# Two graph attention layers in one kernel: the product of a finished block's output is issued between the first and the second group of the next block's sums

## The chip, the cores and the metric

The kernel runs on one core of a Trainium2 chip. The metric is the device time of one execution in microseconds (us). The engines of the core work side by side, each through its own queue in order: TensorE (PE in the profile, with its weight loads as PEld), VectorE (DVE), ScalarE (ACT), GpSimd (POOL) and SyncE (SP, which here only issues DMAs). Transfers between the main memory and the on-chip memory run on 16 DMA engines.

## The reference, cut to what matters

A graph of 6250 nodes with 256 features each and 100,000 edges goes through two residual steps. The first step is two GATv2 layers with 4 heads of 64 channels, with one added edge from each node to itself; the second is one GAT layer with 8 heads of 32 channels. In each layer a node takes a softmax over its incoming edges and sums the rows of the source nodes with these weights.

```python
def _gatv2_layer(x, src, dst, n, Wl, Wr, att, b):
    xl = (x @ Wl).reshape(n, H, C)
    xr = (x @ Wr).reshape(n, H, C)
    e = jax.nn.leaky_relu(xl[src] + xr[dst], NEG_SLOPE)
    logits = jnp.einsum('ehc,hc->eh', e, att)
    ...  # softmax over the edges of each dst: alpha
    msg = xl[src] * alpha[:, :, None]
    out = jax.ops.segment_sum(msg, dst, num_segments=n)
    return out.reshape(n, H * C) + b
...
h = elu(_gatv2_layer(x, src, dst, n, Wl1, Wr1, att1, b1))
h = _gatv2_layer(h, src, dst, n, Wl2, Wr2, att2, b2)
x = _layernorm(x + h)
x = _layernorm(x + _L1_gnn_ref(x, W, a, src, dst))
```

All numbers are 32-bit floats.

## The kernel before, in words

**Blocks.** The nodes are sorted by their number of incoming edges and cut into 49 blocks of 128, one node per partition. Block b has `cols[b]` edge columns: 27 in block 0, 25 in block 1, 18 in block 17, 17 in block 18, 15 in block 27, 11 in blocks 44 and 45, 9 in block 48. With the node's own row a block of layers 1 and 2 has S = `cols[b]` + 1 rows of 260 numbers per partition (block 0 a few more, handled apart). These rows are held in tiles `g` of at most 9 rows each, called groups here: block 0 has four, blocks 1 to 17 have three, and blocks 18 to 48 have two, of equal size or one apart (18 = 9 + 9, 16 = 8 + 8, 12 = 6 + 6). There are 9 such tiles (`rowp`), so GpSimd can load some four blocks of two groups ahead.

**Gathers.** One indirect DMA of GpSimd (line 1300) fetches one edge column: 128 rows of the table in main memory. All three layers take 2409 of them. Layer 2 gathers from the table that layer 1 writes, layer 3 from the table that layer 2 writes. So that a layer can begin its gathers early, the sources of its first three blocks are sorted, and 37 gathers (14, 12 and 11 columns, `soon` in the profile) read the table only up to block 44 (`AHEAD`); the gathers after them need all 49 blocks.

**One block of `layer2`** (lines 1635 to 1666; `i` is 0 in layer 1 and 1 in layer 2). Each engine takes its instructions in the order in which the Python code emits them; the order is written out by hand. In iteration b:

1. `start` issues loads for block b + 3, `gather` the gathers of block b + 1.
2. `ready(b + 1)` makes the block's own terms. In layer 1 (`own1`) TensorE turns the block's input (two transposes, line 1420, copied to SBUF by ScalarE, line 1422) and multiplies it with both weight matrices (`pl` and `pr`, line 1427). In layer 2 (`own2`) both have been loaded, and ScalarE copies `pr` (line 1724).
3. `attend(b)`: VectorE makes the logits, three passes for each group (lines 1591, 1594, 1595; the first pass of the first group was made an iteration earlier). ScalarE puts block b + 1's own row in its tile (line 1684 in layer 1, 1725 in layer 2). `weights` takes the maximum on VectorE (line 1439) and four exponentials on ScalarE (line 1446). Then VectorE makes the first pass of block b + 1 (`first_z`, line 1571), which reads `pr` and that own row.
4. `finish(b - 1)` takes the sums of the block before, `acc`, and returns `rest`, which makes the block's output (layer 1: ELU, lines 1689 to 1697; layer 2: a layer norm, lines 1522 to 1534).
5. `weighted_sum(b)`: VectorE multiplies the rows of each group by their weights (line 1483). Of the last group ScalarE takes some columns in place of VectorE, four multiplies to a column (line 1482): S // 3 of them in layer 1 and S // 2 in layer 2, at most the group's rows less one. TensorE adds the rows up in PSUM by matmuls with the identity (line 1490), two instructions to a row. After the first group's multiply `between` calls `rest`.
6. `last[0]()`: the function that `rest` returned turns the finished output of block b - 1 (transposes on TensorE, the copy of line 1422 on ScalarE), multiplies it with the next layer's weights (line 1427), copies the result to `row` (ScalarE, lines 1704, or 1738 and 1739) and issues the DMAs that write the next layer's table rows (SP, lines 1708 and 1709, or 1740).

Layer 3 uses no TensorE sums; its weighting and adding are on VectorE.

In step 5 ScalarE's multiplies of the last group stand ahead of the copies of step 6 in ScalarE's queue, and all matmuls of the block stand ahead of the transposes of step 6 in TensorE's queue:

```python
for g, (s0, s1) in zip(rows, cut):
    ...
    for t in range(m, n):
        for h in range(H):
            nc.scalar.mul(g4[:, t, h, :], g4[:, t, h, :], by[:, t - m, h : h + 1])
    nc.vector.tensor_mul(...)
    if s0 == 0:
        between()
    for t in range(n):
        nc.tensor.matmul(acc, ident, g4[:, t], ...)
```

Of the kernel before, what the change touches and what calls it, by code (L numbers as in the profile page):

```python
# [26 lines left out]
F32 = mybir.dt.float32  # L27
# [8 lines left out]
P = 128  # L36
# [1171 lines left out]
def tile_by_degree(  # L1208
# [3 lines left out]
    nc = tc.nc  # L1212
    N, F = x.shape
    H2, D2 = att1.shape
    H1, _, D1 = w3.shape
    NB = -(-N // P)
    NP = NB * P
    T = 9
    A1 = F + H1
    W2 = H2 * (D2 + 1)  # L1220
# [5 lines left out]
    xl2_d = dram.tile([NP + 1, W2], F32, name="xl2_d")  # L1226
    xr2_d = dram.tile([NP, W2], F32, name="xr2_d")
    wh_d = dram.tile([NP + 1, A1], F32, name="whs_d")

    def per_head(t, H):  # L1230
        return t.rearrange("p (h d) -> p h d", h=H)
# [55 lines left out]
    s2 = consts.tile([P, NB, H1], F32, name="s2_r")  # L1287
# [129 lines left out]
    def transposed(work, ps, xt):  # L1417
        pt = ps.tile([P, 2, P], F32, name="pt", tag="tp")
        for c in range(2):
            nc.tensor.transpose(pt[:, c, :], xt[:, c * P : (c + 1) * P], ident)  # L1420
        xT = work.tile([P, 2, P], F32, name="xT")
        nc.scalar.copy(xT, pt)  # L1422
        return xT

    def product(pm, xT, w):
        for c in range(2):
            nc.tensor.matmul(pm, xT[:, c, :], w[:, c, :], start=c == 0, stop=c == 1)  # L1427
# [33 lines left out]

        return (wt, None), add_up

    def weighted_sum(work, ps, rows, cut, wts, H, width, between, plus, more=False):


        wt, (k0, k1) = wts
        acc = ps.tile([P, F], F32, name="acc")
        S = cut[-1][1]
        by = None  # L1470
        if k1 > k0:
            by = work.tile([P, k1 - k0, H], F32, name="by")
            nc.scalar.copy(by, wt[:, k0:k1, :])  # L1473
        for k, t in enumerate(plus):
            nc.tensor.matmul(acc, ident, t, start=k == 0, stop=False)
        for g, (s0, s1) in zip(rows, cut):
            n = s1 - s0
            g4 = g[:, :n, : H * width].rearrange("p t (h d) -> p t h d", h=H)[:, :, :, : F // H]
            m = n - by.shape[1] if by is not None and s1 == S else n
# [3 lines that stand above are left out]
            nc.vector.tensor_mul(  # L1483
                g4[:, :m], g4[:, :m],
                wt[:, s0 : s0 + m, :].unsqueeze(3).to_broadcast([P, m, H, F // H]),
# [4 lines that stand above are left out]
                nc.tensor.matmul(  # L1490
                    acc, ident, g4[:, t], start=False, stop=s0 + t == S - 1 and not more
                )
        return acc

    def added_up(work, prod, rows, cut, wts, H, width, between):
# [24 lines left out]
    def spread_of(work, t):  # L1520
        stats = work.tile([P, nc.vector.BN_STATS_DIM], F32, name="stats")
        nc.vector.bn_stats(stats, t)  # L1522
        mv = work.tile([P, nc.vector.BN_AGGR_DIM], F32, name="mv")
        nc.vector.bn_aggr(mv, stats)
        sd = work.tile([P, 2], F32, name="sd")
        nc.scalar.activation(sd[:, :1], mv[:, 1:2], AF.Ln, bias=eps)  # L1526
        nc.scalar.activation(sd[:, :1], sd[:, :1], AF.Exp, scale=-0.5)
        return mv, sd
# [7 lines left out]
    def layer2(i, table, of, width, start, own, finish, follow):  # L1536
# [5 lines left out]
        with ExitStack() as es:  # L1542
            zp = es.enter_context(tc.tile_pool(name=f"z{i}", bufs=1))
            work = es.enter_context(tc.tile_pool(name=f"work{i}", bufs=3))
            ps = es.enter_context(tc.tile_pool(name=f"ps{i}", bufs=2, space=PSUM))
            ps1 = es.enter_context(tc.tile_pool(name=f"ps1{i}", bufs=1, space=PSUM))
            pst = es.enter_context(tc.tile_pool(name=f"pst{i}", bufs=2, space=PSUM))
# [4 lines left out]
            def gather(b):  # L1552
                first = EARLY[b] if b in begun else 0
                rows, cut = begun.pop(b) if first else row_tiles(b, 1)
                gather_rows(b, rows, cut, 1, table, of, width, first, cols[b])
                if b == 0:
                    gather_few(table, i, width)
                state[b] = [rows, cut]
# [3 lines left out]
            def ready(b):  # L1562
                pr, put = own(work, ps, pst, b, state[b][0][0][:, 0, :W2])
                state[b].append(pr)
                later.append(put)
# [68 lines left out]
            acc, rest = None, None  # L1634
            for b in range(NB):
                if b + 3 < NB:
                    start(b + 3)
                if b + 1 < NB:
                    gather(b + 1)
                if b + 2 == NB:  # L1640
                    follow()
                if b + 1 < NB:
                    ready(b + 1)
                rows, cut, wt, new = attend(b)
                if b:
                    rest = finish(work, pst, b - 1, acc)
                else:
                    new()
                    few = few_sum(work, pst, wt[0], cols[0] + 1, H2, D2 + 1)
                if b:  # L1650
                    new()

                last = []

                def between():
                    if b:
                        last.append(rest())

                acc = weighted_sum(
                    work, ps, rows, cut, wt, H2, D2 + 1, between,  # L1660
                    [bias[0]] if i == 0 else [x1[:, b, :], bias[1]], b == 0,
                )
                if b == 0:
                    nc.tensor.matmul(acc, edges_of, few, start=False, stop=True)
                if last:
                    last[0]()
            finish(work, pst, NB - 1, acc)()()

    def none(t):

        nc.vector.memset(t.rearrange("p (h d) -> p h d", h=H2)[:, :, D2:], -BIG)
# [14 lines left out]
    def finish1(work, pst, b, acc):  # L1686
        h = work.tile([P, F], F32, name="h")
        neg = work.tile([P, F], F32, name="neg")
        nc.scalar.activation(neg, acc, AF.Relu, scale=-1.0)
        nc.scalar.activation(neg, neg, AF.Exp, scale=-1.0)  # L1690
        pos = work.tile([P, F], F32, name="pos")
        nc.scalar.activation(pos, acc, AF.Relu)

        def rest():
            row = work.tile([P, 2, W2], F32, name="row2")
            none(row[:, 1, :])
            nc.vector.scalar_tensor_tensor(h, neg, -1.0, pos, op0=OP.add, op1=OP.add)

            def last():
                hT = transposed(work, pst, h)  # L1700
                for j in range(2):
                    pm = pst.tile([P, W2], F32, name="pm", tag="tp")
                    product(pm, hT, wc[1][:, j])
                    nc.scalar.copy(
                        per_head(row[:, j, :], H2)[:, :, : W2 // H2 - j],
                        per_head(pm, H2)[:, :, : W2 // H2 - j],
                    )
                nc.sync.dma_start(xl2_d[b * P : (b + 1) * P], row[:, 0, :])
                nc.sync.dma_start(xr2_d[b * P : (b + 1) * P], row[:, 1, :])

            return last

        return rest

# [12 lines left out]
    def finish2(work, pst, b, h):  # L1727
        mv, sd = spread_of(work, h)

        def rest():  # L1730
            layer_norm(x1[:, b, :], h, mv, sd)

            def last():
                hT = transposed(work, pst, x1[:, b, :])
                pm = pst.tile([P, F + 2 * H1], F32, name="pm3", tag="tp")
                product(pm, hT, wh)
                row = work.tile([P, A1], F32, name="row3")
                nc.scalar.copy(row, pm[:, :A1])
                nc.scalar.copy(s2[:, b, :], pm[:, A1:])
                nc.sync.dma_start(wh_d[b * P : (b + 1) * P], row)  # L1740

            return last

        return rest

# [12 lines left out]
    with ExitStack() as es:  # L1758
        work = es.enter_context(tc.tile_pool(name="work3", bufs=3))
        ps = es.enter_context(tc.tile_pool(name="ps3", bufs=3, space=PSUM))  # L1760
# [59 lines left out]
        acc, den, puts, rest = None, None, {}, None  # L1820
        for b in range(NB):
# [4 lines left out]
            rows, cut, wt, new = attend(b)  # L1826
# [5 lines left out]
            def between():  # L1832
                if b:
                    puts[b - 1] = rest()

            acc = added_up(work, prod, rows, cut, wt, H1, D1, between)
            if b == 0:
                more = ps.tile([P, F], F32, name="few_acc", tag="tp")
# [34 lines left out]
```

## Time and profile before

| | us |
|---|---|
| median of 3 runs (lowest to highest) | 3332.04 (3331.96 to 3335.03) |
| the profiled execution, its own time | 3328.12 |
| its span, first to last instruction | 3326.3 |
| layer 1: first gather to the first `soon` gather of layer 2 | 131 to 1212 |
| layer 2: from there to the first `soon` gather of layer 3 | 1212 to 2236 |
| layer 3: from there to the end | 2236 to 3326 |

| engine | busy us | share of the span | instructions |
|---|---|---|---|
| DVE | 2755.3 | 83% | 2527 |
| POOL | 2435.2 | 73% | 2588 |
| PE | 1416.2 | 43% | 5423 |
| ACT | 1108.0 | 33% | 4428 |

The 2409 gathers take 0.946 us each as POOL's busy time, and 0.30 us lie between two of them, so that one starts every 1.25 us at best. The mean granted clock of TensorE is 0.711 of full speed over the span. A row of a timeline gives the start, the time taken, the engine, the line, the operation, `out<-in`, the number of instructions merged in it, and in brackets the engine's idle time before it with what ended that idle time.

### The profile page before, as it was taken

What the parts mean: (1) busy time and instruction counts of PE and PEld (TensorE: products, weight loads), DVE (VectorE), ACT (ScalarE), POOL (GpSimd) and SP (SyncE); (2) the same over time, 40 slices, a digit from 0 to 9 for tenths busy, and PEclk for the clock granted to TensorE, in tenths of its full rate; (3) what the DMA queues carried; (4) which work ended last, traced back from release to release, by engine and by line L of the source; (5) the groups of instructions that cost most, each with busy time, mean ns of one, the idle gap of its engine ahead of it and who ended that gap; (6) DMA issues with size and microseconds to landing.
All of it is one profiled execution on the core that took longest, in us unless ns stands there. A gap on an engine that the chain in (4) does not pass through costs nothing.

```text
span 3326.3 us, 24261 instructions
## 1 busy us (share of the span) xinstructions
PE 1416.2 (43%) x5423; PEld 1131.0 (34%) x5424; DVE 2755.3 (83%) x2527; ACT 1108.0 (33%) x4428; POOL 2435.2 (73%) x2588
## 2 busy tenths in 40 slices
PE   7346666666677773565656666662000000000000
PEld 5235554555555552454545454552000000000000
DVE  7599998889888888999999999985966767666766
ACT  3134434444444442444445666561000000000000
POOL 5477777777777767777777777767777777777776
PEclk8678888888888886777877878886555555555555
DMA  8744444444444444444444444444333333333333
GB/s 198 145 111 118 117 118 121 118 120 122 121 121 121 124 111 112 122 121 127 121 127 126 132 126 132 131 111 115 108 107 107 108 108 107 108 107 107 107 107 86
DMA packets 189103, 395.84 MB, mean 119 GB/s; under 512 B 56249, under 2 KB 107963, under 8 KB 188934
## 3 DMA queue, kind: packets, MB, share of 16 engines
q0 software_dynamic: 121392, 339.19, 39.0%
q1 hardware_dynamic: 59858, 53.27, 5.7%
q10 hardware_dynamic: 7700, 1.74, 0.5%
q8 instruction: 47, 0.77, 0.1%
q14 instruction: 106, 0.87, 0.1%
HBM read 354.02 MB, written 40.42 MB: 119 GB/s over the span
## 4 chain that ended last, share of the span: by engine, by line
POOL 23%; DVE 15%; issue 13%; PE 7%; DMA 3%; ACT 1%; DVEq 0%; POOLq 0%; ACTq 0%
POOL g L1300 22%; PE acc L1490 6%; DVE g L1483 3%; DVE z L1594 3%; DVE lg L1595 3%; DVE z L1571 3%; DVE z L1591 2%; DMA g<-xl_d,near_r 1%; POOL out L1812 1%; DMA out<-y,node_i 1%; PE pm L1427 1%; DVE stats L1522 0%; DMA g<-whs_d,near_r 0%; ACT sd L1526 0%; DVE weighted L1503 0%
## 5 line engine op out<-in xcount | busy, mean ns | idle before, releaser
L1300 POOL DMA_INDIRECT g<-xl_d,near_r x1569 | 1484.4, 946 | 485.8 <-issue 434.8
L1490 PE MATMUL acc<-g,ident 128*128 128x256 f32 x3408 | 972.0, 455 | 654.2 <-DVE g L1483 357.6
L1490 PEld LDWEIGHTS acc<-g,ident 128*128 128x128 f32 x3408 | 788.8, 235 | 838.3 <-DVE g L1483 378.4
L1300 POOL DMA_INDIRECT g<-whs_d,near_r x766 | 727.1, 949 | 233.3 <-issue 227.2
L1482 ACT ACTIVATE g<-g,by 128x64 f32<-128x64 f32 x2308 | 561.0, 336 | 1.6
L1595 DVE TENSOR_REDUCE lg<-z 128x28 f32<-128x1820 f32 (+4 forms) x234 | 497.4, 2125 | 8.1
L1594 DVE TENSOR_TENSOR z<-z,at 128x1820 f32<-128x1820 f32 (+4 forms) x234 | 496.9, 2124 | 4.7
L1483 DVE TENSOR_TENSOR g<-g,wt 128x1792 f32<-128x1792 f32 (+8 forms) x234 | 331.8, 1435 | 31.9 <-ACT by L1473 31.9
L1512 DVE TENSOR_REDUCE acc_v<-weighted 128x256 f32<-128x4096 f32 (+15 forms) x49 | 343.7, 7014 | 1.6
L1591 DVE TENSOR_TENSOR z<-g,pr 128x1820 f32<-128x1820 f32 (+3 forms) x138 | 299.6, 2171 | 23.2 <-DMA g<-xl_d,near_r 14.8
L1456 ACT ACTIVATE wt<-lg 128x128 f32<-128x128 f32 (+17 forms) x49 | 14.0, 285 | 803.6 <-DVE lg L1455 803.6
L1782 DVE TENSOR_TENSOR lg<-g,s_r 128x56 f32<-128x56 f32 (+4 forms) x111 | 22.4, 214 | 268.5 <-DMA g<-whs_d,near_r 212.2
L1571 DVE TENSOR_TENSOR z<-g,pr 128x2080 f32<-128x2080 f32 (+4 forms) x96 | 197.9, 2061 | 44.5 <-DMA g<-xl_d,near_r 13.5
L1503 DVE TENSOR_TENSOR weighted<-g,wt 128x1792 f32<-128x1792 f32 (+4 forms) x111 | 226.6, 2057 | 0.1
L1422 ACT COPY xT<-pt 128x256 f32<-128x256 f32 x147 | 55.0, 374 | 505.8 <-PE pt L1420 505.8
L1446 ACT ACTIVATE wt<-lg,top 128x19 f32<-128x19 f32 (+14 forms) x392 | 115.7, 295 | 234.2 <-DVE top L1439 224.7
L1427 PE MATMUL pm<-wcat,xT 128*128 128x260 f32 x392 | 99.0, 395 | 22.6 <-ACT xT L1422 22.6
L1427 PEld LDWEIGHTS pm<-wcat,xT 128*128 128x128 f32 x392 | 70.4, 189 | 42.8 <-ACT xT L1422 34.3
L1446 ACT ACTIVATION_READ_ACCUMULATOR wt<-lg,top 128x1 f32 x392 | 73.5, 187 | 0.0
L1812 POOL DMA_INDIRECT out<-y,node_i x49 | 50.1, 1022 | 25.8 <-issue 14.2
L1427 PE MATMUL pm<-wh_cat,xT 128*128 128x272 f32 x196 | 59.0, 424 | 22.6 <-ACT xT L1422 22.6
L1427 PE MATMUL pl<-wcat,xT 128*128 128x260 f32 x196 | 57.2, 415 | 25.2 <-ACT xT L1422 25.2
(250 smaller groups left out, 1527.3 us busy)
## 6 DMA issues: line engine op xcount, KB each, us to landing
g<-xl_d,near_r POOLq DMA_INDIRECT x1569, 2.8
g<-whs_d,near_r POOLq DMA_INDIRECT x766, 2.8
whs_d<-row SPq DMA_DIRECT2D x49, 132.0 KB, 2.0
xl_d<-xl SPq DMA_DIRECT2D x49, 130.0 KB, 7.9
xl_d<-row SPq DMA_DIRECT2D x49, 130.0 KB, 2.6
xr_d<-row SPq DMA_DIRECT2D x49, 130.0 KB, 2.9
two<-xl_d SPq DMA_DIRECT2D x49, 130.0 KB, 2.9
two<-xr_d SPq DMA_DIRECT2D x49, 130.0 KB, 3.3
```

The lines of the kernel that those rows point to most:

```text
L1300: nc.gpsimd.indirect_dma_start(out=g[:, j + own - s0, :width], out_offset=None, in_=table, in_offset=source(of, b, j),)
L1427: nc.tensor.matmul(pm, xT[:, c, :], w[:, c, :], start=c == 0, stop=c == 1)
L1446: nc.scalar.activation(wt[:, :, h], lg[:, :S, h], AF.Exp, bias=top[:, h : h + 1], accum_out=den[:, h : h + 1],)
L1482: nc.scalar.mul(g4[:, t, h, :], g4[:, t, h, :], by[:, t - m, h : h + 1])
L1483: nc.vector.tensor_mul(g4[:, :m], g4[:, :m], wt[:, s0 : s0 + m, :].unsqueeze(3).to_broadcast([P, m, H, F // H]),)
L1490: nc.tensor.matmul(acc, ident, g4[:, t], start=False, stop=s0 + t == S - 1 and not more)
L1503: nc.vector.tensor_mul(prod[:, s0 - base : s1 - base, :].rearrange("p t (h d) -> p t h d", h=H), g[:, :n, :F].rearrange("p t (h d) -> p t ...
L1512: nc.vector.reduce_sum(part, prod[:, : s1 - base, :].rearrange("p s f -> p f s"), axis=AX.X)
L1571: nc.vector.tensor_max(z, rows[0][:, :n, :W2], xr[:, None, :].to_broadcast([P, n, W2]))
L1591: nc.vector.tensor_max(z, g[:, :n, :W2], xr[:, None, :].to_broadcast([P, n, W2]))
L1594: nc.vector.tensor_mul(z, z, at[:, None, :].to_broadcast([P, n, W2]))
L1595: nc.vector.reduce_sum(lg[:, s0:s1, :], z.rearrange("p t (h d) -> p t h d", h=H2), axis=AX.X)
```

## The change

The function that `rest` returned did all of step 6. It is cut in two. The first part, `turn`, holds the transposes, the copy to SBUF and the products; it is called by a new `middle`, which `weighted_sum` calls after the first group's matmuls. The second part, `last`, holds the copies to `row` and the DMAs, and stays where step 6 was, after all groups. In layer 1 each of the two DMAs is now issued directly after its own copy. The last block of a layer calls all parts in turn. No operation is added or removed.

```diff
@@ weighted_sum
+    def weighted_sum(work, ps, rows, cut, wts, H, width, between, middle, plus, more=False):
...
                 nc.tensor.matmul(
                     acc, ident, g4[:, t], start=False, stop=s0 + t == S - 1 and not more
                 )
+            if s0 == 0:
+                middle()
         return acc
@@ layer2
+                def middle():
+                    if b:
+                        last.append(last.pop()())
+
                 acc = weighted_sum(
-                    work, ps, rows, cut, wt, H2, D2 + 1, between,
+                    work, ps, rows, cut, wt, H2, D2 + 1, between, middle,
...
                 if last:
                     last[0]()
-            finish(work, pst, NB - 1, acc)()()
+            finish(work, pst, NB - 1, acc)()()()
@@ finish1
-            def last():
+            def turn():
                 hT = transposed(work, pst, h)
+                made = []
                 for j in range(2):
                     pm = pst.tile([P, W2], F32, name="pm", tag="tp")
                     product(pm, hT, wc[1][:, j])
-                    nc.scalar.copy(
-                        per_head(row[:, j, :], H2)[:, :, : W2 // H2 - j],
-                        per_head(pm, H2)[:, :, : W2 // H2 - j],
-                    )
-                nc.sync.dma_start(xl2_d[b * P : (b + 1) * P], row[:, 0, :])
-                nc.sync.dma_start(xr2_d[b * P : (b + 1) * P], row[:, 1, :])
-
-            return last
+                    made.append(pm)
+
+                def last():
+                    for j, (pm, to) in enumerate(zip(made, (xl2_d, xr2_d))):
+                        nc.scalar.copy(
+                            per_head(row[:, j, :], H2)[:, :, : W2 // H2 - j],
+                            per_head(pm, H2)[:, :, : W2 // H2 - j],
+                        )
+                        nc.sync.dma_start(to[b * P : (b + 1) * P], row[:, j, :])
+
+                return last
+
+            return turn
@@ finish2
-            def last():
+            def turn():
                 hT = transposed(work, pst, x1[:, b, :])
                 pm = pst.tile([P, F + 2 * H1], F32, name="pm3", tag="tp")
                 product(pm, hT, wh)
-                row = work.tile([P, A1], F32, name="row3")
-                nc.scalar.copy(row, pm[:, :A1])
-                nc.scalar.copy(s2[:, b, :], pm[:, A1:])
-                nc.sync.dma_start(wh_d[b * P : (b + 1) * P], row)
-
-            return last
+
+                def last():
+                    row = work.tile([P, A1], F32, name="row3")
+                    nc.scalar.copy(row, pm[:, :A1])
+                    nc.scalar.copy(s2[:, b, :], pm[:, A1:])
+                    nc.sync.dma_start(wh_d[b * P : (b + 1) * P], row)
+
+                return last
+
+            return turn
```

More of the change, by code (lines that the diff above doesn't have):

```diff
@@ L1462, in weights @@
         return (wt, None), add_up
-    def weighted_sum(work, ps, rows, cut, wts, H, width, between, plus, more=False):
+    def weighted_sum(work, ps, rows, cut, wts, H, width, between, middle, plus, more=False):
         wt, (k0, k1) = wts
```

## The prediction

> **What bounds the kernel now.** I read the page's groups first, then POOL's waits. The page's costliest group is the gathers; its columns are busy time, mean ns of one, and the idle time before them with what ended it.
>
> ```profile
> L1300 POOL DMA_INDIRECT g<-xl_d,near_r x1569 | 1484.4, 946 | 485.8 <-issue 434.8
> ```
>
> All 2409 gathers at 0.946 + 0.30 us make 3.0 ms of the 3.3 ms span, so GpSimd nearly never rests. What another engine costs must show as a wait of GpSimd. In its waits (total us, times, longest), "issue" is only the steady 0.30 us; two single waits stand out:
>
> ```profile
> POOL g L1300 <- PE pl L1427: 17.2, 2, 16.9
> ...
> POOL g L1300 <- DVE stats L1522: 14.1, 3, 13.5
> ```
>
> The timeline places them at 1211.98 and 2235.97: each is the first `soon` gather of the next layer, which needs block 44's table row. The names of the releasers are inferred; the row itself is on SP, 2.7 us before:
>
> ```profile
> 2233.26 0.32 SPq L1740 DMA_DIRECT2D whs_d<-row  x1
> ...
> 2235.97 0.95 POOL L1300 DMA_INDIRECT g<-whs_d,soon  x1 [13.48 <-DVE stats L1522]
> ```
>
> With 2.5 us at 1260.69 (block 48's row) and 3.7 us at 1302.81 (a free tile), GpSimd waits 36.6 us for the other engines after its start. That is the most that any speed-up here can give; a slow-down is not limited. Layer 3 starts when block 44's row of layer 2 lands, and gathers without a break after that. So the question is when that row lands.
>
> The table by stages (length; PE, PEld, DVE, ACT, POOL busy; clock) tells who sets that: layer 1 from block 27, layer 2's three-group blocks, its two-group blocks, layer 3.
>
> ```profile
> 850.00:1244.00 394.00, 278.14 (x1044) 220.30 (x1044) 331.17 (x293) 187.71 (x764) 285.39 (x302) 0.86 0.45 119
> 1292.00:1736.00 444.00, 257.17 (x960) 208.26 (x960) 430.88 (x324) 185.84 (x765) 333.41 (x353) 0.78 0.45 122
> 1736.00:2236.00 500.00, 319.52 (x1142) 253.75 (x1142) 468.78 (x395) 301.45 (x1252) 368.01 (x391) 0.80 0.47 127
> 2282.00:3326.00 1044.00, 2.68 (x6) 1.50 (x6) 730.59 (x772) 68.00 (x197) 778.49 (x819) 0.50 0.39 106
> ```
>
> In layer 2 VectorE is busy 97% and 94% of the time, and a block's gathers end 24 to 39 us before its weights are ready (timeline, block by block), so GpSimd's lead is not used up: VectorE's chain sets layer 2, and each microsecond added to it arrives at 2235.97. In layer 1 VectorE waits about 2 us a block for TensorE (line 1671, 45.7 us in 20 waits): there TensorE's chain sets the pace. VectorE's waits in layer 2's two-group blocks:
>
> ```profile
> DVE g L1483 <- ACT by L1473: 9.9, 29, 0.4
> DVE z L1571 <- ACT g L1725: 8.5, 13, 1.5
> DVE z L1571 <- DMA g<-xl_d,near_r: 5.7, 5, 1.4
> ```
>
> Only line 1571, which needs ScalarE's copy of line 1725, can change. ScalarE's timeline of one block (27), whose sums run on TensorE from 1914.96 to 1924.58 and whose transposes follow at 1924.42, shows how near that copy is:
>
> ```profile
> 1915.53 6.78 ACT L1482 ACTIVATE g<-g,by 128x64 f32<-128x64 f32 x28
> 1924.83 0.37 ACT L1422 COPY xT<-pt 128x256 f32<-128x256 f32 x1 [2.52 <-PE pt L1420]
> 1926.48 0.38 ACT L1738 COPY row<-pm 128x264 f32<-128x264 f32 x1 [1.27 <-PE pm L1427]
> 1926.76 0.17 ACT L1739 COPY s_r<-pm 128x8 f32<-128x8 f32 x1
> 1926.81 0.40 ACT L1724 COPY pr<-two 128x260 f32<-128x260 f32 x1
> 1927.12 0.42 ACT L1725 COPY g<-two 128x260 f32<-128x260 f32 x1
> ```
>
> and on VectorE:
>
> ```profile
> 1926.98 0.27 DVE L1439 TENSOR_REDUCE top<-lg 128x4 f32<-128x64 f32 x1
> 1927.58 2.32 DVE L1571 TENSOR_TENSOR z<-g,pr 128x2080 f32<-128x2080 f32 x1 [0.33 <-ACT g L1725]
> ```
>
> ScalarE weights from 1915.5 to 1922.3 beside the sums, then stands idle 2.5 us for the transposes. That idle time is the cover of the weighting. The copy of line 1725 ends at 1927.54, 0.2 us after VectorE could use it (line 1439's end + 0.1).
>
> **The change, part by part.** No work comes or goes; two queues are reordered.
>
> *ScalarE, layer 2.* The copy of line 1422 moves ahead of the last group's multiplies. It waits for transposes that stand behind the first group's matmuls; 28 multiplies, two `row` copies, `pr` and the copy of line 1725 queue behind it. How long the first group takes is read from the sums' rows (PE busy, PEld busy, then PEclk):
>
> ```profile
> 1914.90:1919.70 4.80, 4.74 (x11) 3.81 (x12) 0.50 0.39 100
> 1919.90:1924.30 4.40, 4.40 (x22) 3.78 (x20) 0.99 0.37 97
> ```
>
> The sums begin at half clock, 0.427 us an instruction, and change to 0.216 us. Over all blocks that takes 2.7 to 6.1 us, about 4.4: nearly always inside the first group. Here the first group's 16 instructions end 6.0 us after the start at 1914.96, not at half of 9.6. Then: 0.42 to the copy (1924.42 to 1924.83), 0.32 to the first multiply (spacing of ScalarE's short copies), 28 x 0.2425 = 6.8 (6.78 for 28), 1.1 from the last multiply to the end of line 1725's copy (1926.48 to 1927.54, and 0.04). Sum 6.0 + 0.42 + 0.32 + 6.8 + 1.1 = 14.6; now it is 12.6. VectorE is ready at 12.4, so it waits 2.3 instead of 0.2: **2.1 us lost** in this block.
>
> The same sum with each block's own rows, blocks 18 to 45: S 18: 2.4 (4 blocks), 17: 2.2 (5), 16: 1.9 (5), 15: 1.8 (5), 14: 1.5 (4), 13: 1.5 (3), 12: 1.0 (2); together 9.6 + 11 + 9.5 + 9 + 6 + 4.5 + 2 = 51.6 us. Longer blocks meet the clock at other points: its change falls on a fixed grid of 3.41 us (the first fast matmuls of 45 blocks lie within 0.3 us of it). Played forward block by block on that grid, the loss is 44 to 48, depending on the start; I take 46. Without the change the same replay ends 0.1 us from the trace's last block.
>
> Three-group blocks lose nothing: block 10's copy would end 12.6 us after the sums begin, VectorE needs it at 18.7. Their cover is the third group's passes on VectorE (lines 1591, 1594 and 1595, 1.78 to 2.05 us each); where it is gone, from block 18 on, the loss begins.
>
> *TensorE, layer 2.* Transposes and products go first; the second group then runs at ScalarE's pace (0.97 a row against 0.43). `acc` is done some 4 us later, still 2 us ahead of line 1522. The second group's tile is released as much later; GpSimd is 24 us or more ahead.
>
> *Layer 1.* TensorE's chain to `pr` keeps its length: sums, two transposes, the 0.46 us for ScalarE's copy, products (2.0), own transposes, `pl`, `pr`. ScalarE must weight before TensorE needs its rows: with S 16 the last of 20 multiplies (0.32 + 4.88) ends 5.2 us after the copy starts, and TensorE asks for that row after 0.43 + 2.0 + 7 x 0.43 = 5.4. The slack is 0.2 to 1 over the blocks; only S 18 lacks some 0.2, where the gathers still set the pace. Both PSUM buffers of the turned tiles stay taken until the `row` copies: the first copy ends 0.4 us after the multiplies, TensorE's last row as late, so the next transposes lose nothing. Gain: the copy of block b + 1's input no longer stands behind `row` copies that wait for products (0.51 against 0.46 idle of TensorE), 0.08 over 20 blocks, and 0.35 at block 48, whose ELU waits for those copies now (1253.61): **-2 us**. What is late next there is TensorE itself.
>
> *SP and the rows.* The DMAs stay where they were; in layer 1 each already left right after its own copy (1209.27 and 1210.15). Loads of block b + 4 behind line 1740 start 2 us later and are needed two blocks on. Block 48's row shifts 1.7 us more than block 44's and has 1.1 of slack before 2282.23: +0.6.
>
> *Transposes and the clock.* No row shows a transpose inside the slow stretch followed by the products. A pause there could cost nothing, or one more grid step at half speed (3.4 us, 1.7 of work) in layer 1 blocks whose first group has six rows or fewer (6 blocks, about a third of them): 0 to +3. I take 0, since larger groups have reached full clock before. The Trainium skill (TensorE: Matmul & The Clock Gate, Part 4: PE-mode transpose) says that transposes do not count as TensorE activity for the clock; by that rule the +3 would be due, as an estimate.
>
> **Sum**: 3328.1 (the profiled execution) + 46 - 2 + 0.6 = 3372.7. The median shown is 3.9 above that execution, so **3376.6**, 1.3% slower.
>
> **The rivals.**
> *Warm start.* If TensorE came to a block without a long pause, the first group would take 16 x 0.216 = 3.5, and line 1725 would end at 3.5 + 8.6 = 12.1, before 12.4: no loss, and the 13 us of present waits (8.5 and 5.7, less the part due to gathers) go too: 3332 - 13 - 2 = 3317, faster. It decides where the pause before the sums falls under 3.6 us: the last blocks of layer 1 (3.5 to 3.8) show 0 to 7 slow matmuls. I work out pauses of 4.3 to 5.4; layer 1 has 4.1 to 5.3 and is always slow at the start. 6%.
> *It changes nothing*: layer 2 would absorb the wait, if GpSimd's gathers held VectorE. Against it: 94% busy and the lead of 24 us. 3332, 4%.
> *Half the loss*: ScalarE's queue drains quicker than its rows say, or full clock always comes at 2.7 us instead of 4.4: 1.7 us sooner, so 0.85 us less at half speed in each of 28 blocks, 3376.6 - 24 = 3352. 10%.
> *Layer 1 loses too*: the slack of 0.2 is missed by 0.5 to 1 us in 20 blocks: 3377 + 15 = 3392. 10%.
> *Forecast* (44 to 48, -7 to +3 in layer 1): 3365 to 3385, 70%.
>
> The range holds the forecast, most of the half loss and layer 1's loss: 3350 to 3393. A measurement of this kernel tells about 0.2% (7 us) from no change: faster 0.06, same 0.04, slower 0.9.
>
> **What would show it.** Right: in layer 2's two-group blocks ScalarE idle about 5 us before line 1422 and multiplies that begin after it; line 1571 waiting 1.3 to 2.9 us for line 1725; GpSimd's wait near 2236 grown to about 58 us or spread over the tiles' releases; layer 1's first `soon` gather within 3 us of 1212. Wrong: the sums at full clock from their start, or multiplies that begin before line 1422's copy, or line 1671's waits grown.

## The result, and the profile after

The change makes the kernel slower by what was forecast: 3375.3 us (median of 4, 3374.8 to 3376.7) against 3333.5 us (median of 4, 3332.0 to 3335.1), a ratio of 1.0126 with the 95% interval [1.0108, 1.0143]. The forecast was 3376.6 us.

The profiled execution took 3376.74 us with a span of 3374.9 us, 48.6 us more than the one of before; the medians lie 41.8 us apart. So some 7 us of the difference between the two profiled executions are scatter, and 3 of them stand in layer 3, in which nothing changed.

The stages again (length; PE, PEld, DVE, ACT, POOL busy; clock). The third is longer, 550 against 500 us, because it is cut where block 44's row lands:

```profile
850.00:1244.00 394.00, 279.12 (x1042) 219.35 (x1041) 330.92 (x293) 182.59 (x762) 285.10 (x301) 0.85 0.46 120
1292.00:1736.00 444.00, 255.14 (x962) 206.91 (x962) 430.15 (x327) 184.13 (x765) 332.69 (x351) 0.78 0.45 120
1736.00:2286.00 550.00, 357.37 (x1149) 238.21 (x1149) 478.15 (x404) 300.22 (x1264) 376.80 (x399) 0.87 0.44 117
2331.00:3375.00 1044.00, 2.68 (x6) 1.50 (x6) 730.86 (x772) 67.99 (x197) 778.80 (x817) 0.50 0.39 106
```

In the other three stages VectorE and GpSimd are busy as long as before, to within 1 us. In layer 2's two-group blocks VectorE is busy 87% of the time, where it was 94%. VectorE's waits in that stage (total us, times, longest) tell what it waits for:

```profile
DVE z L1573 <- ACT g L1737: 44.5, 23, 3.1
DVE z L1573 <- DMA g<-xl_d,near_r: 10.5, 5, 2.9
DVE g L1483 <- ACT by L1473: 9.9, 29, 0.4
```

Line 1573 is now `first_z`, line 1737 the copy of the block's own row. That wait was 8.5 us; the one put down to a DMA was 5.7, and the one for `by` is as it was. ScalarE's waits of the same stage show why the copy is late: the copy of the turned tile waits 5.1 us on average over 28 blocks, 2.1 before, and the multiplies queue behind it. The first line is of the profile of before, the second of the one after:

```profile
ACT xT L1422 <- PE pt L1420: 59.0, 28, 3.0
ACT xT L1422 <- PE pt L1420: 142.8, 28, 6.6
```

Block 27, the block that the prediction took apart, on TensorE:

```profile
1935.17 5.34 PE L1490 MATMUL acc<-g,ident 128*128 128x256 f32 x16 [5.25 <-DVE g L1483]
1940.35 0.38 PE L1420 MATMUL pt<-ident,near_r 128*128 128x128 f32 x2
```

on ScalarE:

```profile
1940.77 0.37 ACT L1422 COPY xT<-pt 128x256 f32<-128x256 f32 x1 [4.93 <-PE pt L1420]
1941.04 6.79 ACT L1482 ACTIVATE g<-g,by 128x64 f32<-128x64 f32 x28
1947.73 0.36 ACT L1752 COPY row<-pm 128x264 f32<-128x264 f32 x1
1947.99 0.16 ACT L1753 COPY s_r<-pm 128x8 f32<-128x8 f32 x1
1948.05 0.38 ACT L1736 COPY pr<-two 128x260 f32<-128x260 f32 x1
1948.36 0.41 ACT L1737 COPY g<-two 128x260 f32<-128x260 f32 x1
```

and on VectorE, ready at 1947.47 and kept for 1.34 us:

```profile
1947.20 0.27 DVE L1439 TENSOR_REDUCE top<-lg 128x4 f32<-128x64 f32 x1
1948.81 2.32 DVE L1573 TENSOR_TENSOR z<-g,pr 128x2080 f32<-128x2080 f32 x1 [1.34 <-ACT g L1737]
```

Before, ScalarE weighted from 1915.5 to 1922.3 beside the sums and then waited for the transposes. Now it waits first and weights afterwards, and VectorE comes to the end of that chain before it is done.

The delay reaches GpSimd where the prediction said, as one wait for block 44's row and as releases of tiles (waits in the same stage):

```profile
POOL g L1300 <- PE pt L1420: 30.7, 12, 4.8
POOL g L1300 <- DVE wt L1452: 19.5, 1, 19.5
```

The first `soon` gather of layer 3 starts at 2281.75, 45.8 us later than before; that of layer 2 at 1216.6, 4.6 us later, of which 1.1 were there at the very first gather. The prediction's sign that layer 1 is unharmed, this gather within 3 us of 1212, was thus missed.

### The profile page after: what moved, and what is told of

The parts are those of the page before. It is cut to its first block, busy times and chain, and to the rows that moved or that the text cites. A ratio compares the mean times of both kernels' runs of the same rounds, so it can differ in the third digit from the quotient of the medians.

```text
span 3374.9 us, 24354 instructions
## 1 busy us (share of the span) xinstructions
PE 1456.8 (43%) x5423; PEld 1111.7 (33%) x5424; DVE 2755.6 (82%) x2527; ACT 1091.1 (32%) x4428; POOL 2443.6 (72%) x2588
## 3 DMA queue, kind: packets, MB, share of 16 engines
q0 software_dynamic: 121392, 339.19, 38.7%
## 4 chain that ended last, share of the span: by engine, by line
POOL 20%; DVE 15%; issue 12%; PE 6%; ACT 6%; DMA 3%; DVEq 0%; POOLq 0%; ACTq 0%
POOL g L1300 19%; PE acc L1490 6%; ACT g L1482 5%; DVE g L1483 3%; DVE z L1573 3%; DVE z L1596 2%; DVE lg L1597 2%; DVE z L1593 2%; DMA g<-xl_d,near_r 1%; DMA out<-y,node_i 1%; POOL out L1828 1%; DVE stats L1524 1%; DMA g<-whs_d,near_r 1%; DVE weighted L1505 0%; ACT sd L1528 0%
## 5 line engine op out<-in xcount | busy, mean ns | idle before, releaser
L1490 PE MATMUL acc<-g,ident 128*128 128x256 f32 x3408 | 1023.8, 458 | 661.6 <-DVE g L1483 328.0
L1490 PEld LDWEIGHTS acc<-g,ident 128*128 128x128 f32 x3408 | 765.1, 232 | 902.2 <-DVE g L1483 348.7
L1597 DVE TENSOR_REDUCE lg<-z 128x28 f32<-128x1820 f32 (+4 forms) x234 | 497.3, 2125 | 8.1
```

The costliest lines, as they stand in the source:

```text
L1490: nc.tensor.matmul(acc, ident, g4[:, t], start=False, stop=s0 + t == S - 1 and not more)
L1597: nc.vector.reduce_sum(lg[:, s0:s1, :], z.rearrange("p t (h d) -> p t h d", h=H2), axis=AX.X)
```

## The experiments

The theory: the loss is ScalarE's order in layer 2, the turned copy ahead of the weighting. The rivals: both layers pay alike; or the turn behind the first sums costs TensorE's time whatever ScalarE does; or the sums' slow clock is what makes the turn late.

All 12 runs fell on three chips on which the kernel before takes 3866 to 3923 us, where it took 3332 in the runs of the result ("the first runs" from here on; whether their chip is among the three is not known). So the absolute times that the first four expectations name could not come out; a run is compared with the kernel before of its own set, and stages with stages. The sets:

| run | set | this, us | before in the set, us | ratio, 95% interval |
|---|---|---|---|---|
| `e1_layer1_only` | A | 3906.1 | 3866.8 | 1.0118 [1.0078, 1.0157] |
| `e2_layer2_only` | A | 3914.8 | 3866.8 | 1.0125 [1.0083, 1.0168] |
| `e3_weighting_first` | A | 3853.7 | 3866.8 | 0.9965 [0.9926, 1.0004] |
| `e4_change_no_pause` | A | 3931.0 | 3866.8 | 1.0184 [1.0142, 1.0225] |
| `e5_layer1_again` | B | 3982.0 | 3922.5 | 1.0160 [1.0112, 1.0209] |
| `e6_layer2_again` | B | 4015.5 | 3922.5 | 1.0256 [1.0208, 1.0304] |
| `e7_weighting_first_again` | B | 3900.3 | 3922.5 | 0.9957 [0.9925, 0.9990] |
| `e8_no_pause_again` | B | 4090.5 | 3922.5 | 1.0434 [1.0384, 1.0485] |
| `e9_before_control` | C | 3894.2 | 3897.2 | 0.9982 [0.9952, 1.0012] |
| `e10_weighting_first_third` | C | 3869.1 | 3897.2 | 0.9939 [0.9914, 0.9963] |
| `e11_layer1_third` | D | 3906.8 | 3866.4 | 1.0111 [1.0061, 1.0161] |
| `e12_whole_change` | D | 3951.3 | 3866.4 | 1.0232 [1.0189, 1.0276] |

A and C are one chip, whose kernel before differs by 0.8% between the two sets.

What carries the verdicts is one table from the traces. For the two stages of two-group blocks (layer 1 from the reciprocal of line 1451 of block 27 to that of block 45; layer 2 from block 18 to 44) it gives the length and VectorE's idle time, added up by the instruction that comes after it (the largest places; first-pass is `first_z` with its semaphore instruction, in layer 1 also the padding of `pr` right ahead of it, line 1671 or 1677 in the kernels before and after, where the wait there stands; multiply is line 1483, reciprocal line 1451, statistics the first use of `acc` by VectorE). All in us:

| profiled execution | layer 1 length | its idle before first-pass | layer 2 length | first-pass | multiply | reciprocal | statistics |
|---|---|---|---|---|---|---|---|
| before, first runs | 348.1 | 41.8 | 469.5 | 11.5 | 8.8 | 0 | 0 |
| after, first runs | 346.4 | 40.0 | 507.3 | 49.9 | 8.8 | 0 | 0 |
| `e9_before_control` | 361.1 | 54.7 | 520.4 | 62.9 | 8.8 | 0 | 0 |
| `e1_layer1_only` | 402.7 | 96.5 | 524.3 | 66.7 | 8.8 | 0 | 0 |
| `e2_layer2_only` | 355.7 | 49.4 | 562.2 | 51.2 | 40.3 | 20.5 | 0 |
| `e12_whole_change` | 399.3 | 93.0 | 571.9 | 71.8 | 31.7 | 18.6 | 0 |
| `e3_weighting_first` | 361.9 | 55.6 | 525.0 | 24.4 | 8.8 | 0 | 40.7 |
| `e10_weighting_first_third` | 366.4 | 60.1 | 532.0 | 26.5 | 8.8 | 0 | 45.6 |

### One layer alone

```diff
                 def middle():
-                    if b:
+                    if b and i == 0:
                         last.append(last.pop()())
...
                 if last:
-                    last[0]()
+                    (last[0] if i == 0 else last[0]())()
```

for layer 1 alone; `i == 1` for layer 2 alone.

> The first part (transposes, copy, products) moves behind the first group in layer 1 alone; layer 2 keeps the order of before. Theory (the loss comes from ScalarE's weighting queued behind the copy of line 1422 in layer 2's two-group blocks): within 6 us of before, 3330 to 3340, with VectorE's waits of line 1571 in layer 2 back at some 13 us. Rival (turning a block's output between two groups delays TensorE's sums, in either layer): about half of the 42 us, 3350 to 3360.

> The same move in layer 2 alone. Theory: nearly all of the loss, 3370 to 3378. Rival (either layer loses alike): 3350 to 3360.

In set A layer 1 alone costs 39 us and layer 2 alone 48 us. The two are each other's control. In layer 2's stage the layer 2 edit makes 562.2 out of 524.3 us, +38, as much as the change made in the first runs (469.5 to 507.3, +37.8). So the price in layer 2 comes out at the same size, though at other places: before `first_z` VectorE idles no longer than with the old order there (51.2 against 66.7 us), and the added time stands before the multiply and the reciprocal, which need ScalarE's queue as well. But in layer 1's stage the layer 1 edit makes 402.7 out of 355.7 us, +47, where the first runs show -1.7. On these chips the theory's "layer 1 is free" is wrong, and the rival is nearer.

> The edit of the layer 1 run once more, because that set ran on a chip on which the kernel before took 3867 us as well, and gathers waited for transfers there. All figures as differences from the kernel before in the same set, where that kernel takes about 3330 us. Theory (the price lies in layer 2, where VectorE waits for ScalarE's weighting): -2 to +6 us; the first soon gather of layer 2's rows within 5 us of the kernel before, and VectorE's waits for ScalarE's weighting in layer 2 (first_z behind line 1482's rows) at most 5 us. Rival (both layers pay alike): +18 to +25 us, spread over blocks 18 to 45 of layer 1.

> The edit of the layer 2 run once more. Differences from the kernel before in the same set. Theory: +36 to +46 us, with VectorE's wait for ScalarE's weighting in layer 2 at 40 to 50 us and layer 1 unchanged to within 2 us. Rival (both layers pay alike): +18 to +25 us.

The same on another chip: +59 and +93 us. Both prices are larger there; the theory's -2 to +6 for layer 1 fails again, +93 lies far above its +36 to +46 for layer 2, and the rival's +18 to +25 fits neither half.

> The edit of the layer 1 run a third time, beside the whole change. Where the kernel before takes about 3330 us: theory (the price lies in layer 2) -2 to +6 us against the kernel before of the set, rival (both layers pay alike) +18 to +25 us. Where it takes about 3900 us: +40 to +60 us as in the two sets before, by the theory that gathers have no lead there, so that a later end of a block's sums holds GpSimd in layer 1 too: GpSimd's waits behind TensorE are over 100 us longer in layer 1 than with the weighting first.

> The change itself, as it stands, in the same set as its layer 1 half. Where the kernel before takes about 3330 us: +42 us. Where it takes about 3900 us: if the two halves pay each for itself, the sum of the two halves of the earlier sets, +85 to +155 us; if they share one limit (GpSimd can be held only once), +45 to +70 us, little above one half.

Layer 1 alone costs 40 us and the whole change 85 us. The halves of set A add up to 87: each pays for itself, and a shared limit (45 to 70) is out. The theory given for it, that GpSimd lacks a lead on these chips, fell too. In layer 1's blocks 26 to 44 the last gather of a block is issued 56 to 70 us before the block's reciprocal in `e9_before_control` and 64 to 82 us before it in `e12_whole_change`, against 15 to 39 us in the first runs. GpSimd waits at the first gather of a second group, three blocks or more ahead, for a tile nine groups back: in `e5_layer1_again` that of block 34 starts at 1194.55, and the first group's sums of block 30 end at 1194.28. Its waits are a consequence there, not the cause. Behind TensorE it waits 111 us in that stage of `e11_layer1_third` and 58 in `e10_weighting_first_third`, some 52 us more and not the 100 expected.

These 18 blocks are not all of layer 1. Its three stretches in the profiled executions of these chips, between the reciprocals of the blocks named (us; in the first runs they take 476 and 477, 195 and 197, 348 and 346 before and after):

| layer 1 has | profiled executions | blocks 0 to 18 | 18 to 27 | 27 to 45 |
|---|---|---|---|---|
| the order of before | `e9`, `e2`, `e6` | 699.4, 668.9, 695.2 | 224.4, 225.8, 224.7 | 361.1, 355.7, 364.5 |
| the change | `e1`, `e11`, `e12`, `e5` | 611.8, 618.4, 622.5, 625.4 | 254.0, 258.0, 255.5, 297.8 | 402.7, 403.5, 399.3, 433.8 |
| the weighting first (next section) | `e3`, `e10`, `e7` | 660.0, 660.7, 652.6 | 231.4, 232.9, 238.4 | 361.9, 366.4, 362.8 |

So these chips lose most, some 200 us against the first runs, in the three-group blocks of layer 1, where the change gains 43 us or more; behind block 18 it loses at least 28 and then 35 us. Read with these single executions, the 39 to 60 us that layer 1 alone costs in the medians are what remains of a gain and two losses.

### The weighting first

ScalarE's multiplies are put ahead of `middle`, so that ScalarE has its old order, while TensorE keeps the turn behind the first group's sums:

```diff
+        def by_scalar():
...
+            for t in range(n - k, n):
+                for h in range(H):
+                    nc.scalar.mul(g4[:, t, h, :], g4[:, t, h, :], by[:, t - n + k, h : h + 1])
         for g, (s0, s1) in zip(rows, cut):
...
-            for t in range(m, n):
-                for h in range(H):
-                    nc.scalar.mul(g4[:, t, h, :], g4[:, t, h, :], by[:, t - m, h : h + 1])
+            if s1 == S and s0 == 0:
+                by_scalar()
...
             if s0 == 0:
                 between()
+                if s1 < S:
+                    by_scalar()
```

> The whole change, but ScalarE's multiplies of the last group are issued after the first group's multiply of VectorE, ahead of the copy of line 1422; TensorE's order is that of the changed kernel. Theory: the multiplies run beside the first group again and end 7.4 us after the sums begin in block 27; then the copy (0.4), the products (1.2) and the copies up to line 1725 (1.1) end near 10.2, before VectorE's 12.4. The loss goes and so do the present waits of line 1571 (some 13 us): 3315 to 3325. Rival (TensorE's order is what costs): it stays at 3370 to 3378.

> Weighting before the turned copy, run once more. Differences from the kernel before in the same set. Theory (ScalarE's order, copy ahead of weighting, is the whole loss): the loss of layer 2 goes, VectorE's wait for the weighting falls under 10 us, and the time is -18 to +3 us. Rival (the turn and its product behind the sums cost TensorE or PSUM time whatever ScalarE's order): still +35 us or more.

> Weighting before the turned copy, a third time. Differences from the kernel before in the same set. Theory (ScalarE's order is the loss): -25 to +3 us, first soon gather of layer 3's data earlier than in the control or within 3 us. Rival (the turn behind the sums costs TensorE time whatever ScalarE's order): +35 us or more.

Three sets give 13, 22 and 28 us less than before; the intervals of the last two lie below 1, and their gains are a little more than the theory's -18 and -25. The rival, that the turn costs TensorE's time whatever ScalarE's order, is out in all three. And the table by stages says where: the idle time that the change adds goes in both stages. In layer 2 the waits before the multiply and the reciprocal, both of which need ScalarE's queue, are back at 8.8 and 0, and layer 1's wait is back at 56 to 60. So ScalarE's order is the cause of the loss in blocks 27 to 45 of layer 1 on these chips too. In layer 2 a new wait takes the place of part of the old one: VectorE waits 41 to 46 us for `acc`, whose last rows now come behind products that wait for ScalarE. VectorE's waits of this stage in `e3_weighting_first`:

```profile
DVE stats L1535 <- PE acc L1475: 17.2, 7, 3.3
DVE stats L1535 <- PE acc L1501: 13.2, 7, 2.6
DVE z L1584 <- ACT pr L1747: 12.7, 2, 12.2
```

The stage is therefore no shorter than the control's. What is gained stands elsewhere. The profiled executions of `e10_weighting_first_third` and of the control lie 22 us apart: blocks 0 to 18 of layer 1 are 38.7 us shorter (the three executions with the old order there differ by 30 among themselves), the stretch from block 45 of layer 1 to block 0 of layer 2 takes 112.0 us against 121.6, that from block 44 to 48 of layer 2 80.7 against 87.3; the four other stretches of the two layers are 31 us longer together.

For comparison the waits of `e2_layer2_only`, where ScalarE's order is the change's:

```profile
DVE z L1573 <- DMA g<-xl_d,near_r: 33.1, 15, 3.4
DVE g L1483 <- ACT by L1473: 18.3, 14, 2.4
DVE g L1483 <- remote: 17.9, 7, 3.1
DVE den L1451 <- ACT sd L1528: 12.7, 6, 3.0
```

"remote" stands where the profile finds no instruction that ended the wait. In the traces of these chips it is a frequent entry; they hold some 12,000 to 14,000 semaphore events where those of the first runs hold 53,000. I therefore rest on lengths and idle times, not on these names.

### No pause ahead of the sums

The change with 8 or 9 more matmuls of the bias term (an extra load on TensorE, whose result the next matmul overwrites) ahead of each block's sums:

```diff
+        if not more:
+            for k in range(WARM[len(plus) - 1]):
+                nc.tensor.matmul(acc, ident, plus[-1], start=True, stop=True)
         for k, t in enumerate(plus):
             nc.tensor.matmul(acc, ident, t, start=k == 0, stop=False)
```

> The whole change, and TensorE gets 8 (layer 1) or 9 (layer 2) extra matmuls with the identity ahead of each block's sums, into the accumulator that the first real one overwrites: 3.5 to 3.9 us of work in a pause of 5 to 6 us, so that the sums begin at full clock. Theory with the clock in it: the first group takes 3.5 us instead of 6, line 1725's copy ends at 12.1 in block 27, VectorE waits no more in layer 2, and layer 1's waits for TensorE (some 2 us a block) shrink too: 3297 to 3315. Rival (the first group's length has no part in it): 3370 to 3378, or more by the extra work.

> The change with matmuls ahead of the sums so that TensorE does not pause, run once more. Differences from the kernel before in the same set. Theory (the turn comes late because the sums ahead of it run at half clock): the first group's sums end 2 us earlier per block, the wait for the weighting falls under 15 us and the time is between -35 and -10 us. Rival (the sums' clock does not matter to the turn, or the matmuls added take what the clock gives): +40 us or more.

+64 and +168 us: the theory's gain did not come, and in set B the kernel is slower than both halves together (59 + 93). But the edit did not do what it was made for. Two blocks of layer 2 in `e4_change_no_pause` on TensorE:

```profile
2308.02 4.05 PE L1477 MATMUL acc<-fixed_r,ident 128*128 128x256 f32 x18
2311.91 0.59 PE L1479 MATMUL acc<-near_r,ident 128*128 128x256 f32 x2
2312.34 0.59 PE L1479 MATMUL acc<-fixed_r,ident 128*128 128x256 f32 x2
2318.66 6.67 PE L1494 MATMUL acc<-g,ident 128*128 128x256 f32 x16 [5.72 <-issue]
```

The added matmuls (line 1477) need nothing and run at once after the last block, at full clock; then TensorE pauses 5.7 us for the weighted rows all the same, and 16 instructions take 6.67 us, half clock throughout. So it goes in blocks 20 to 27, after pauses of 5.0 to 6.8 us; 12 of the 26 blocks of that stage run the first eight instructions of their sums at full clock, after pauses of at most 1.9 us. Six of these, blocks 38 to 43, take 99.8 us together, and 99.8 in `e8_no_pause_again`, where they are at full clock too, against 102.8 in `e12_whole_change` and, with the old order in layer 2, 100.0 in `e9_before_control` and 107.5 in `e11_layer1_third`: too close to tell. So the run does not say what the change would cost at full clock. The rival of a warm start stays open: to test it, matmuls would have to stand in the pause itself, behind a wait that ends in it.

### The kernel before as a control

> The kernel before itself, run as if it were a change, to have its trace from the same chip as the others of the set. Both theories: ratio 1.000 within the interval. On a chip on which it takes about 3870 to 3920 us, the theory that transfers are what is slower there expects GpSimd to wait for landed data and for freed tiles in layers 1 and 2, against 36.6 us of waits in the profile of before, and a layer 3 of gathers at about 1.36 us each against 1.25 us; the rival (all engines slower) expects VectorE's and ScalarE's instructions to take longer by the same ratio.

The ratio is 0.9982 [0.9952, 1.0012]: nothing moved. Of the two theories of what is slow on these chips neither holds as it stood. VectorE's and ScalarE's instructions take what they took (line 1595's reduction 2125 ns in both, ScalarE's multiply 338 against 336 ns), so it isn't all engines. But ScalarE's multiplies no longer follow one another without a break; in the page of before and in the one of `e9_before_control`:

```profile
L1482 ACT ACTIVATE g<-g,by 128x64 f32<-128x64 f32 x2308 | 561.0, 336 | 1.6
L1482 ACT ACTIVATE g<-g,by 128x64 f32<-128x64 f32 x2308 | 610.6, 338 | 360.2 <-issue 353.2
```

257 multiplies of the control that follow another multiply and wait for no semaphore start only after an idle time of over 0.5 us, mostly 1.0 to 1.1 us, 274 us in all; in the first runs none does. So on these chips ScalarE at times stands still with nothing to wait for. Why, no run shows.

Layer 3's gathers are slower, 1.04 us busy on average (766 of `e6_layer2_again`) against 0.95, and 1.40 us apart in long stretches against 1.25; in `e9_before_control`:

```profile
3026.49 1.10 POOL L1300 DMA_INDIRECT g<-whs_d,near_r  x1 [0.30 <-issue]
3027.89 1.10 POOL L1300 DMA_INDIRECT g<-whs_d,near_r  x1 [0.30 <-issue]
3029.29 1.11 POOL L1300 DMA_INDIRECT g<-whs_d,near_r  x1 [0.30 <-issue]
```

But in the two-group blocks of layer 1 GpSimd is further ahead than in the first runs, and a gather's packets end about as long after its start (in the DMA records of block 34 some 2.3 us after it for most, in `e5_layer1_again` as in before). So transfers are not what VectorE waits for there.

## Why the prediction was right, point by point

- **What bounds the kernel, and where a delay would arrive.** Right: layer 2's two-group stage takes 37.8 us more, VectorE's idle time before `first_z` in it 38.4 us more, and layer 3 starts 45.8 us later.
- **The 46 us of layer 2.** Right in mechanism, a little too large: 37.8 us to block 44 and 2.6 more to block 48. In block 27 the chain behind the transposes is as summed (0.42 + 0.27 + 6.79 + 0.94 us measured, 0.42 + 0.32 + 6.8 + 1.1 forecast); what was oversized is the first group, 5.2 us from its start to the transposes instead of 6.0. Over blocks 18 to 44 the first fast instruction came 3.96 us after the sums' start, against 4.59 in the profile of before. Half of 0.63 us in 26 blocks is 8 us, about the difference to the forecast; that this is the cause is worked out, not tested.
- **Three-group blocks lose nothing.** Right: layer 2 from block 0 to block 18 takes 444.5 us before and after, and no block differs by more than 0.01 us.
- **Layer 1, -2 us.** The step that failed, if by little: from block 0's reciprocal to that of block 0 of layer 2 it is 3.9 us more. Blocks 0 to 18 lose 0.9 us and blocks 18 to 27 2.3, of which the forecast had only "S 18 lacks some 0.2"; the layer's end loses 2.5 us instead of gaining 0.35; blocks 27 to 45 gain 1.7. The forecast's gain of 0.08 a block was also more than its own rows give: TensorE's idle times of 0.517 and 0.462 us there make 0.055.
- **The sum.** The terms were 46 - 2 + 0.6 on a profiled execution that lay 3.9 us under its median. In the profiled executions 1.2 us (at the start) + 3.9 + 40.4 + 3.0 (layer 3) make the 48.5 us; the medians differ by 41.8. That the forecast lies only 1.3 us from the measured median is in part luck: layer 2 was put some 6 us too high and layer 1 5.9 too low.
- **Transposes and the clock.** Taken as 0, with 0 to +3 as the bounds. In layer 1's blocks 27 to 45 nothing is lost, and where the transposes themselves still ran slowly, the products behind them ran at full clock:

```profile
1133.86 5.49 PE L1490 MATMUL acc<-g,ident 128*128 128x256 f32 x12 [4.08 <-DVE row L1677]
1139.14 0.63 PE L1420 MATMUL pt<-ident,h 128*128 128x128 f32 x2
1140.24 2.02 PE L1427 MATMUL pm<-wcat,xT 128*128 128x260 f32 x8 [0.46 <-ACT xT L1422]
```

  The 8 instructions take 2.02 us here as in the other blocks. The rule of the Trainium skill (TensorE: Matmul & The Clock Gate, Part 4: PE-mode transpose), that transposes don't count as activity for the clock, is not put to the test by this row: the granted clock was 0.5 from 1132.95 to 1139.78, and the sums filled that stretch from 1133.86 on but for the transposes' last 0.63 us.
- **Rivals.** "It changes nothing" and "half the loss" are out by the result. "Layer 1 loses too" is out for the runs of the result, but is what the later three chips show, with another size than the one named: not a slack missed by 0.5 to 1 us, but 38 to 47 us more of VectorE's waiting ahead of `first_z` in 18 blocks (69 in set B), and a gain in the three-group blocks. "Warm start" was not tested where the loss is.

What stays open is why these chips are slower. In layer 1 VectorE waits there for TensorE, which reports late. The wait stands before the padding of `pr`; block 31 of `e12_whole_change`, on TensorE and on VectorE:

```profile
1148.95 1.04 PE L1427 MATMUL pr<-wcat,xT 128*128 128x260 f32 x4
1154.90 0.06 DVE L1677 MEMSET pr<- 128x4 f32 x1 [6.30 <-remote]
```

In 17 of the 18 blocks 28 to 45 of that run VectorE goes on over 1 us after the end that the trace gives for the product into `pr` (median 3.3 us), in the first runs 0.08 us after it. But in 16 of these 17 the trace holds an update of the semaphore that TensorE's instructions raise, 0.06 to 0.07 us before VectorE goes on (here at 1154.84). The lateness is not the change's alone. With the order of before in layer 1 (`e9`, `e2`, `e6`) it stands in 15 or 16 of the blocks 1 to 18, with medians of about 10 us, and in none of the blocks 28 to 45. With the change it is in none of the first and in 17 of the second; with the weighting first in none and in 2. So ScalarE's order decides whether it comes in blocks 28 to 45, and the turn behind the first group's sums ends it in blocks 1 to 18. How, and why TensorE is late at all, no run shows. Nor was the weighting-first kernel, the fastest of all here, run under the conditions of the first runs.

## What to carry to other kernels

When a copy that must wait is moved ahead of work that need not, that work loses the cover of the wait, and "wait + work" lands on whoever reads the queue's last output. Decide the order on each engine by itself: here TensorE's early turn was no harm, and only ScalarE's early copy was. A price of zero that rests on a slack of 0.2 to 1 us holds only where that slack does: layer 1 cost 4 us in the first runs and 40 to 60 on three chips later, where it was no longer free in blocks 18 to 45.

## What the runs showed of the hardware that was not expected

- The same program took 3332 us in the first runs and 3866 to 3923 us on three chips later, with VectorE's instructions equally long and ScalarE's to about 1%. Of the extra time some 200 us lie in blocks 0 to 18 of layer 1. On one chip the kernel before moved by 0.8% from set to set.
- TensorE's sums begin at half clock after a pause (0.427 us an instruction, later 0.216): in the kernel before after 4.1 us of pause in blocks 41 to 44 of layer 1, and in `e4_change_no_pause` after 5.7 us although 18 matmuls had run at full clock just ahead of it.
- A block's period may lock to the clock's grid: in the profile after, the reciprocals of layer 2's blocks 23 to 27 follow each other by 20.44, 20.47, 20.47 and 20.47 us, six times the 3.413 us of the grid on which the clock changes; before, the same periods were 19.31, 19.10, 19.11 and 18.31. That the grid holds them is read from these rows, not tested.
